# Accounting for ScalarE in the order of issue of a chain of Mamba layers

## The chip, the cores and the metric

The kernel runs on one core of one Trainium2 chip. The core has five engines with a queue each: TensorE (PE, with its weight loads shown as PEld), VectorE (DVE), ScalarE (ACT), GpSimd (POOL) and SyncE (SP, which here issues nearly all DMAs). The metric is the device time of one execution in microseconds (us); lower is better. Before the change it is 10859.94 us, the median of three runs (10855.66 to 10861.70).

## The reference

Four layers run one after the other on an input of 4 images, 192 channels, 64 x 64 pixels, all in float32.

- Layer 0: each image is 4096 tokens of 192 channels. They are normalised (mean and variance over the 192 channels, then scale and bias). Two Mamba blocks take the result, one of them with the channels reversed, and `out = xs + y1 + y2`.
- Layer 1: a layer norm, one Mamba block and a residual, then a depthwise 3 x 3 convolution with batch norm and gelu, a second layer norm and an MLP (192 to 768 to 192).
- Layer 2: a masked 3 x 3 depthwise convolution with weights made from the image means.
- Layer 3: a layer norm, a sedenion product in windows of 4 x 4 pixels, and an MLP.

A Mamba block is, in short:

```
xc, z = split(x @ in_w.T)                     # 384 channels each
xc = silu(conv1d(xc, conv_w) + conv_b)        # 4 taps (3 in layer 1)
dt, B, C = split(xc @ x_w.T)                  # 12, 16 and 16 columns
dt = softplus(dt @ dt_w.T + dt_b)
h[t] = exp(dt[t] * A) * h[t-1] + dt[t] * xc[t] * B[t]     # 16 states per channel
y = sum over the states of h[t] * C[t], + D * xc
out = (y * silu(z)) @ out_w.T
```

## The kernel before

**Tiles and units.** Tokens are cut into tiles of 512 (T), so there are 32 tiles. One tile of one Mamba block is a unit: layer 0 has 64 (the two blocks take turns), layer 1 has 32. The 384 channels by 16 states of a unit are laid out as 12 groups (k, 0 to 11) of 4 pieces (j) of 128 rows. So a unit is 48 scans, and the 48 scans of all units make one long stream. `Scans.run` goes through the stream one scan at a time; such a step is called a tick here.

**What a tick issues.** `Scans.step` puts out, for scan i: the decay two scans ahead (`decay`, L613: ACT computes `exp(dt * A)` into one of three PSUM tiles dA), and the scan itself (`step`, L619, DVE). After the last scan of a group (j = 3), `read` first copies the last column of h into the state kept for the next tile, and then multiplies h by C on POOL (L635). The state is copied by ACT in layer 0 (L632) and by POOL in layer 1 (L634). The next group's `product` follows (L606, dt * xc times B): DVE does it, except for groups 3, 7 and 11 of layer 0 ("shared"), which POOL does into buffers named h_apart. Some ticks later PE sums the states (`sum`, L644), and DVE takes the sums (`skip`, L667 in layer 0, L669 in layer 1). h has three buffers, h_apart two.

**All other work** runs behind the scans and is ordered by `Behind`. It holds lanes, queues of generators; each `yield Piece(...)` says what the next piece needs: time on PE (`pe`), ticks to wait (`wait`), flags that must be set (`after`), a PSUM bank (`bank`; two exist), or that it is a burst. A burst is an activation that needs another table than Exp (Silu, Softplus, Gelu), so that a table load stands before it and another one before the next decay. Bursts are let out only at an edge: the decay just issued is the last of a group and a product by DVE follows. At each tick `issue` first puts out evictions from PSUM that are due (2 ticks after the matmul for ACT in layer 0, 1 in layer 1; 3 and 2 for DVE); then the lanes are tried in order, as long as a budget of PE time per tick (`tile`: 1.85 in layer 0, 2.1 in layer 1) is above zero. Unused budget is not kept. `force` puts out everything that can go, with no regard to budget, until a condition holds: rows of dt in DRAM before they are loaded, C before the read, the gate's silu and a free y before `skip`.

**Layer 0's lanes.** Lane 0 spreads B and C. Lane 1 runs the fronts (`Mamba.front`): in_w product into raw, convolution (`convolve`) into xc, Silu burst (L471), x_w product, dt, Softplus burst (L495), dt and dt * xc to DRAM, z and its Silu burst (L513). xc has two buffers for both blocks together, so the convolution of a unit waits until the unit two places before it has done its `skip`. Lane 2 runs `back` (out_w, L871 to L888). Lane 3 runs `norm`: `bn_stats` and `bn_aggr` on DVE (L828, L829), four small POOL instructions for 1/sigma and shift (L832 to L835), four ACT passes of 128 x 192 (L839) and the transposes into xT, evicted by ACT (L853).

**Layer 1's lanes.** Lane 0: C and `back`. Lane 1: fronts (`sum_taps` replaces the convolution: three ACT evictions per projection, L559) and the first norm (`NormT.run`). Lane 2: `tail` with the depthwise convolution (L1101), its Gelu burst (L1120) and the second norm. Lane 3: the MLP (`MlpT.run`), with six evictions (L364), a Gelu burst over 3072 columns (L371) and the second product (L378). A tail waits for the MLP of three tiles before, and a back for that tile's second norm.

Layers 2 and 3 run from about 8960 us on with another scheduler (`Lanes`), which the diff leaves alone. `drain` issues what is left of layer 0 and layer 1 after their last scan.

Of the kernel before, what the change touches and what calls it, by code (L numbers as in the profile page):

```python
# [22 lines left out]
C = 192  # L23
# [141 lines left out]
class Piece:  # L165
# [4 lines left out]
    def __init__(self, pe=0.0, wait=0, after=(), burst=False, bank=False, lock=False):  # L170
        self.pe, self.wait, self.after, self.burst = pe, wait, after, burst
        self.bank, self.lock = bank, lock


class Behind:
# [4 lines left out]

    BANKS = 2

    def __init__(self, psum, tile, act, dve, lanes=4):
        self.psum, self.tile, self.act, self.dve = psum, tile, act, dve
        self.lanes = [deque() for _ in range(lanes)]
# [12 lines left out]
    def later(self, fn, dve=False, bank=True, more=0):  # L198
        done = [False]
        self.pending.append((self.now + (self.dve if dve else self.act) + more, fn, done, bank))  # L200
        return done

    def issue(self, everything=False):
        keep = []
        for entry in self.pending:
            due, fn, done, bank = entry
            if everything or due <= self.now:
                fn()
                done[0] = True
                self.held -= bank  # L210
            else:
# [3 lines left out]
    def try_lane(self, n, edge, force=False, idle=True):  # L215
# [11 lines left out]
        if not force and (self.now < self.ready[n] or (p.burst and not edge)):  # L227
            return None
        self.locked |= p.lock
# [9 lines left out]
    def tick(self, edge):  # L239
        self.now += 1  # L240
        self.issue()
# [13 lines left out]
    def force(self, until):  # L255
        while not until():
            self.now += 1
            self.issue(True)
# [3 lines left out]
    def drain(self, beside=lambda: None):  # L262

        while any(self.lanes) or self.pending:
# [4 lines left out]
class NormT:  # L269
# [15 lines left out]
    def run(self, x, g, b, d, which):  # L285
# [11 lines left out]
        yield Piece(after=[h], wait=3, lock=True)  # L297
# [20 lines left out]
        h = behind.later(power)  # L318
# [16 lines left out]
        yield Piece(after=[h], wait=3)  # L335
        for k in range(2):
            nc.scalar.activation(  # L337
# [4 lines left out]
class MlpT:  # L342
# [6 lines left out]
    def run(self, x, taken, last):  # L349
# [20 lines left out]
        yield Piece(after=made, burst=True)  # L370
# [31 lines left out]
class Mamba:  # L402
# [42 lines left out]
    def front(self, xn, first, u):  # L445
# [48 lines left out]
        yield Piece(after=halves, burst=True)  # L494
# [8 lines left out]
        yield Piece(1.7, bank=True, after=u["free"][1:])  # L503
# [8 lines left out]
        yield Piece(after=made, burst=True)  # L512
# [3 lines left out]
    def convolve(self, raw, project, u):  # L516
# [25 lines left out]
        yield Piece(after=halves, burst=True)  # L542

    def sum_taps(self, raw, projected, u):
# [3 lines left out]
        for d in range(ND):  # L548
            yield Piece(1.7, bank=True, after=u["free"][:1])
            if d == 0:  # L550
                xc = u["xc"] = self.work.tile([128, ND, T], F32, name="xc", bufs=2)
# [17 lines left out]
        yield Piece(burst=True, wait=4)  # L569
# [110 lines left out]
class Scans:  # L680
# [107 lines left out]
def two_mambas(tc, x, gb_ap, m_ins, ex_aps, out, at_first):  # L788
# [3 lines left out]
    with ExitStack() as ctx:  # L792
# [14 lines left out]
        behind = Behind(psum, 1.85, 2, 3)  # L807
# [12 lines left out]
        def norm(u):  # L820
            xt = u["x"]
            stats = work.tile([128, nq, 6], F32, name="stats")
            mv = work.tile([128, nq, 2], F32, name="mv")
            rs = work.tile([128, nq], F32, name="rs")
            for q in range(nq):
                if q == 2:
                    yield Piece(wait=1)
                nc.vector.bn_stats(stats[:, q, :], xt[:, q, :])  # L828
                nc.vector.bn_aggr(mv[:, q, :], stats[:, q, :])  # L829
            yield Piece(wait=1)  # L830
# [986 lines left out]
```

## Time and profile before

| | |
|---|---|
| median of three runs | 10859.94 us |
| the profiled execution, its own time | 10861.64 us |
| its span, first to last instruction | 10859.9 us |
| mean granted TensorE clock | 0.818 |
| layer 0's scans | 79 to 5321 us |
| layer 1's scans | 5418 to 8926 us |
| layers 2 and 3 | from about 8957 us |

| stretch of the span, us | PE | DVE | ACT | POOL busy |
|---|---|---|---|---|
| 82 to 5295 | 4257 | 5066 | 3535 | 4605 |
| 5430 to 8936 | 3025 | 2974 | 2282 | 2379 |
| 9200 to 10860 | 1442 | 833 | 667 | 171 |

All is of one profiled execution. Lines begin with the line of the kernel (L613), the engine and the operation; `out<-in` are the program's names for the tiles, then come shapes and the number of instructions, busy time in us, the mean duration of one in ns, and the idle time of the engine just before them with what ended it. ACT_TABLE_LOAD is a table load of ACT. PEclk is the share of its full clock that PE was granted.

### The profile page before, as it was taken

The page shows a single profiled execution, that of the slowest core. Times are in us where ns is not written, and L with a number is a line of the kernel's source. Part 1 is how long each engine was busy: PE and PEld are TensorE (multiplying, and loading weights), DVE is VectorE, ACT ScalarE, POOL GpSimd, SP SyncE. Part 2 cuts the span into 40 slices and gives each one's busy share as a digit, 9 for nine tenths or more (in the row PEclk, how much of TensorE's full clock was granted, in tenths as well). Part 3 has the DMA queues.
Part 4 walks back from the last instruction along what each step waited for, and adds up shares of the span by engine and source line. Part 5 has one row for each costly group of instructions (what it writes and reads, how often), then busy time and mean ns, then how long its engine had stood idle before and what let it go on. Part 6 is the DMA issues. An engine that isn't in the chain of part 4 may idle for free. (4 is left out here: it accounts for less than half of the span.)

```text
span 10859.9 us, 96522 instructions
## 1 busy us (share of the span) xinstructions
PE 9009.0 (83%) x30776; PEld 3561.5 (33%) x30776; DVE 9102.4 (84%) x7953; ACT 6632.6 (61%) x9880; POOL 7240.8 (67%) x2816
## 2 busy tenths in 40 slices
PE   7888888888888887887678889889888986889898
PEld 2222222222222222222223333333333323455455
DVE  8999999999999999999698888888888885555552
ACT  5666666666666666666466666666666653444443
POOL 6888888888888888888676666666676661111100
PEclk7777777777777777777678988888898887899999
DMA  6666666666666666666454545554454443112110
GB/s 170 174 181 179 174 182 176 174 182 177 177 180 181 177 175 184 175 178 181 128 149 129 140 128 135 138 134 135 131 145 129 132 110 81 41 50 64 43 40 18
DMA packets 969557, 1515.08 MB, mean 140 GB/s; under 512 B 244346, under 2 KB 277150, under 8 KB 968534
## 3 DMA queue, kind: packets, MB, share of 16 engines
q1 hardware_dynamic: 968190, 1505.85, 52.0%
q8 instruction: 243, 3.98, 0.2%
q10 hardware_dynamic: 856, 3.05, 0.1%
q14 instruction: 268, 2.20, 0.1%
HBM read 1295.45 MB, written 213.12 MB: 139 GB/s over the span
## 5 line engine op out<-in xcount | busy, mean ns | idle before, releaser
L619 DVE TENSOR_TENSOR_SCAN h<-dA,m_state,h 128x512 f32<-128x512 f32 x3840 | 4673.6, 1266 | 409.6 <-ACT dA L613 345.9
L635 POOL TENSOR_TENSOR h<-h,C 128x2048 f32<-128x2048 f32 x960 | 4347.4, 4534 | 605.3 <-ACT m_state L632 500.8
L613 ACT ACTIVATE dA<-dtE,m_A 128x512 f32<-128x512 f32 x4608 | 3108.4, 687 | 1468.6 <-DVE h L619 1370.2
L606 DVE TENSOR_TENSOR h<-dtxE,B 128x2048 f32<-128x2048 f32 x960 | 2169.4, 2260 | 67.1 <-DMA dtxE<-r_dtx 67.1
L644 PE MATMUL y<-h,gather 128*32 128x512 f32 x7680 | 1271.7, 740 | 472.4 <-POOL h L635 395.2
L1352 POOL TENSOR_TENSOR d<-d,rs 128x512 f32<-128x512 f32 x64 | 86.1, 1345 | 1613.2 <-DVE rs L1351 1592.7
L457 PE MATMUL ps_in<-xT,m_in_w 96*128 96x512 f32 x1536 | 942.1, 761 | 241.6 <-ACT raw L464 126.4
L619 DVE TENSOR_TENSOR_SCAN h_apart<-dA,m_state,h_apart 128x512 f32<-128x512 f32 x768 | 922.2, 1259 | 40.2 <-ACT dA L613 40.2
L606 POOL TENSOR_TENSOR h_apart<-dtxE,Bs 128x2048 f32<-128x2048 f32 x192 | 892.9, 4651 | 6.0 <-ACT Bs L595 6.0
L635 POOL TENSOR_TENSOR h_apart<-h_apart,C 128x2048 f32<-128x2048 f32 x192 | 870.7, 4535 | 38.7 <-ACT m_state L632 37.4
L531 PE MATMUL ps_conv<-raw,m_conv 128*128 128x512 f32 x1536 | 727.9, 625 | 0.0
L634 POOL COPY m_state<-h 128x4 f32<-128x4 f32 x384 | 71.9, 187 | 931.1 <-DVE h L619 891.4
L457 PE MATMUL ps_in<-xn,m_in_w 96*128 96x512 f32 x768 | 473.1, 767 | 230.4 <-ACT xc L559 148.2
L457 PEld LDWEIGHTS ps_in<-xT,m_in_w 96*128 96x128 f32 x1536 | 351.7, 242 | 811.5 <-issue 419.5
L644 PEld LDWEIGHTS y<-h,gather 128*32 128x32 f32 x7680 | 164.3, 116 | 1268.6 <-POOL h L635 582.2
L1101 PE MATMUL ps_dw<-strip,dw 96*96 96x512 f32 x1152 | 529.6, 609 | 1.6 <-ACT x L1110 0.9
L475 PE MATMUL ps_x<-xc,m_pack 128*44 128x512 f32 x576 | 353.2, 762 | 204.6 <-ACT xc L471 197.7
L1517 PE MATMUL sed_ps<-xn,sed 64*128 64x256 f32 (+3 forms) x2944 | 486.7, 404 | 7.0 <-DVE y L1536 7.0
L531 PEld LDWEIGHTS ps_conv<-raw,m_conv 128*128 128x128 f32 x1536 | 312.5, 207 | 449.4 <-issue 419.7
L613 ACT ACT_TABLE_LOAD x345 | 442.6, 1283 | 14.7 <-DMA dtE<-r_dt 8.6
L359 PE MATMUL ps_h<-xn,t 96*128 96x512 f32 x768 | 429.6, 715 | 15.0 <-ACT xn L337 9.8
L378 PE MATMUL ps_o<-hid,t 128*96 128x512 f32 x768 | 403.8, 673 | 27.5 <-ACT hid L371 23.3
(201 smaller groups left out, 12458.2 us busy)
## 6 DMA issues: line engine op xcount, KB each, us to landing
dtE<-r_dt SPq DMA_DIRECT2D x2304, 256.0 KB, 5.0
dtxE<-r_dtx SPq DMA_DIRECT2D x2304, 256.0 KB, 4.2
r_dt<-dt SPq DMA_DIRECT2D x96, 768.0 KB, 4.0
r_dtx<-raw SPq DMA_DIRECT2D x96, 768.0 KB, 5.4
x<-x SPq DMA_DIRECT2D x64, 384.0 KB, 3.9
img<-x SPq DMA_DIRECT2D x28, 512.0 KB, 8.3
xt<-in_x SPq DMA_DIRECT2D x32, 384.0 KB, 5.6
x<-o SPq DMA_DIRECT2D x32, 384.0 KB, 5.0
```

The source lines that it names most:

```text
L359: nc.tensor.matmul(ps, self.w1[:, k, bass.ts(m, 128)], x[:, k, :], start=(k == 0), stop=(k == 1))
L378: nc.tensor.matmul(ps, self.w2[:, m, bass.ts(k, CP)], h[:, m, :], start=(m == 0), stop=(m == NH - 1),)
L457: nc.tensor.matmul(ps, self.in_w[:, k, bass.ts(e, 128)], xn[:, k, :], start=(k == 0), stop=(k == 1))
L475: nc.tensor.matmul(ps, self.x_w[:, d, :], xc[:, d, :], start=(d == 0), stop=(d == ND - 1))
L531: nc.tensor.matmul(ps, self.conv[:, d, j, :], raw[:, d, j : j + T], start=(j == 0), stop=(j == K - 1))
L606: engine.tensor_tensor(h, u["rows", k // 2, 1], u[B, k % 2].unsqueeze(1).broadcast_to([128, 4, T]), ALU.mult)
L613: self.nc.scalar.activation(dA, u["rows", k // 2, 0][:, j, :], AF.Exp, scale=self.A[:, k, j : j + 1])
L619: self.nc.vector.tensor_tensor_scan(h[:, j, :], u.pop(("dA", k, j)), h[:, j, :], self.state[:, k, j : j + 1], ALU.mult, ALU.add,)
L635: nc.gpsimd.tensor_tensor(h, h, u["C", k % 2].unsqueeze(1).broadcast_to([128, 4, T]), ALU.mult)
L644: self.nc.tensor.matmul(u["ys"][32 * j : 32 * j + 32, :], self.ex.gather[:, i // 2, :], h[:, j, :], start=(i == 0), stop=(i == 3 and not s ...
L1101: nc.tensor.matmul(ps, dw[:, k, j, :], s[:, k, dy : dy + rows, dx : dx + HW], start=(j == 0), stop=(j == 8),)
L1517: nc.tensor.matmul(out, sed[p, int(h is not None), i ^ position(k, s), cols], xn[b, g][p, c, :], start=group(t) not in begun, stop=left[gr ...
```

## The change

- **An account of ScalarE.** `Behind` gets `spare`, the ACT time that a tick leaves free (1.0 in layer 0, 1.4 in layer 1; 0.7 more in `drain`). `left` rises by `spare` at each tick and never stands above it. Each ACT piece and eviction has a cost `act`, which is taken off. An ACT eviction that is due goes out only while `left` is above zero. A burst needs at least 0.6 of `spare`; another ACT piece needs its cost, or must be under 0.6 of `spare`.
- **Bursts first.** At an edge, one waiting burst is tried before the evictions that are due; before, the evictions came first.
- **PE's budget** per tick goes from 1.85 to 1.6 in layer 0 and from 2.1 to 1.8 in layer 1.
- **Layer 0's norm** takes its sums on ACT: four Identity passes that accumulate the sum, a POOL instruction that makes the negative mean, four Square passes with it as bias that accumulate the squares, three POOL instructions, and the four passes as before. `bn_stats` and `bn_aggr` go. Each pass is a piece of its own with a wait of one tick.
- **The state** is copied by POOL in layer 0 too.
- **xc** has three buffers: a convolution waits for the skip of the unit three places before. z keeps two.
- In the second part of `NormT.run`, each of the two last ACT passes is a piece.

```diff
-    def later(self, fn, dve=False, bank=True, more=0):
+    def later(self, fn, dve=False, bank=True, more=0, act=0.65):
         done = [False]
-        self.pending.append((self.now + (self.dve if dve else self.act) + more, fn, done, bank))
+        due = self.now + (self.dve if dve else self.act) + more
+        self.pending.append((due, fn, done, bank, 0.0 if dve else act))
         return done
 
     def issue(self, everything=False):
         keep = []
         for entry in self.pending:
-            due, fn, done, bank = entry
-            if everything or due <= self.now:
+            due, fn, done, bank, act = entry
+            if everything or due <= self.now and (not act or self.left > 0):
                 fn()
                 done[0] = True
                 self.held -= bank
+                self.left -= act
...
-        if not force and (self.now < self.ready[n] or (p.burst and not edge)):
+        if not force and (
+            self.now < self.ready[n]
+            or (p.burst and not (edge and self.left >= 0.6 * self.spare))
+            or (not p.burst and p.act > max(self.left, 0.6 * self.spare))
+        ):
             return None
+        self.left -= p.act
...
     def tick(self, edge):
         self.now += 1
+        self.left = min(self.left + self.spare, self.spare)
+        if edge:
+            for n in range(len(self.lanes)):
+                if self.says[n] and self.says[n].burst and self.try_lane(n, True):
+                    edge = False
+                    break
         self.issue()
...
     def force(self, until):
         while not until():
             self.now += 1
+            self.left = self.spare
             self.issue(True)
...
     def drain(self, beside=lambda: None):
 
+        self.spare += 0.7
...
-        yield Piece(after=[h], wait=3, lock=True)
+        yield Piece(after=[h], wait=3, act=1.05, lock=True)
...
-        h = behind.later(power)
+        h = behind.later(power, act=0.25)
...
-        yield Piece(after=[h], wait=3)
         for k in range(2):
+            yield Piece(after=[h], wait=0 if k else 3, act=0.8)
...
-        yield Piece(after=made, burst=True)
+        yield Piece(after=made, burst=True, act=5.3)
         nc.scalar.activation(h, h, AF.Gelu)
...
-        yield Piece(after=halves, burst=True)
+        yield Piece(after=halves, burst=True, act=4.1)
         nc.scalar.activation(dt, dt, AF.Softplus)
...
-        yield Piece(1.7, bank=True, after=u["free"][1:])
+        yield Piece(1.7, bank=True, after=u["z_free"])
...
-                    yield Piece(1.7 if j < K - 1 else 0.85, bank=j == 0, after=made + u["free"][:1])
+                    yield Piece(1.7 if j < K - 1 else 0.85, bank=j == 0, after=made + u["xc_free"])
                 if d == j == 0:
-                    xc = u["xc"] = self.work.tile([128, ND, T], F32, name="xc", bufs=2)
+                    xc = u["xc"] = self.work.tile([128, ND, T], F32, name="xc", bufs=3)
...
-        if self.shared:
-            nc.scalar.copy(self.state[:, k, :], h[:, :, T - 1])
-        else:
-            nc.gpsimd.tensor_copy(self.state[:, k, :], h[:, :, T - 1])
+        nc.gpsimd.tensor_copy(self.state[:, k, :], h[:, :, T - 1])
...
-            before = units[n - 2][1] if n > 1 else None
-            unit[1]["free"] = [before["skipped"], before["gated"]] if before else []
+            unit[1]["xc_free"] = [units[n - 3][1]["skipped"]] if n > 2 else []
+            unit[1]["z_free"] = [units[n - 2][1]["gated"]] if n > 1 else []
...
-        behind = Behind(psum, 1.85, 2, 3)
+        behind = Behind(psum, 1.6, 2, 3, 1.0)
...
-            for q in range(nq):
-                if q == 2:
-                    yield Piece(wait=1)
-                nc.vector.bn_stats(stats[:, q, :], xt[:, q, :])
-                nc.vector.bn_aggr(mv[:, q, :], stats[:, q, :])
...
+            def passes(func, sums=None, **args):
+                for q in range(nq):
+                    yield Piece(wait=1, act=0.55)
+                    more = {n: v[:, q : q + 1] for n, v in args.items()}
+                    if sums is not None:
+                        more["accum_out"] = sums[:, q : q + 1]
+                    nc.scalar.activation(xs[:, q, :], xt[:, q, :], func, **more)
+
+            yield from passes(AF.Identity, shift)
+            yield Piece(wait=2)
+            nc.gpsimd.tensor_scalar(shift, shift, -1.0 / C, None, ALU.mult)
+            yield Piece(wait=2)
+            yield from passes(AF.Square, rs, bias=shift)
+            yield Piece(wait=2)
+            nc.gpsimd.tensor_scalar(rs, rs, 1.0 / C, EPS, ALU.mult, ALU.add)
             nc.gpsimd.tensor_tensor(rs, rs, minus_half, ALU.pow)
-            nc.gpsimd.tensor_tensor(shift, mv[:, :, 0], rs, ALU.mult)
-            nc.gpsimd.tensor_scalar(shift, shift, -1.0, None, ALU.mult)
+            nc.gpsimd.tensor_tensor(shift, shift, rs, ALU.mult)
             yield Piece(wait=3)
...
+            yield from passes(AF.Identity, scale=rs, bias=shift)
...
-        behind = Behind(psum, 2.1, 1, 2)
+        behind = Behind(psum, 1.8, 1, 2, 1.4)
...
-            yield Piece(after=made, burst=True)
+            yield Piece(after=made, burst=True, act=3.6)
             nc.scalar.activation(x2, x2, AF.Gelu)
```

The two Silu bursts get `act=4.1` in the same way, and `sum_taps` the three buffers.

More of the change, by code (lines that the diff above doesn't have):

```diff
@@ L165, with __init__ @@
 class Piece:
-    def __init__(self, pe=0.0, wait=0, after=(), burst=False, bank=False, lock=False):
+    def __init__(self, pe=0.0, wait=0, after=(), act=0.0, burst=False, bank=False, lock=False):
         self.pe, self.wait, self.after, self.burst = pe, wait, after, burst
-        self.bank, self.lock = bank, lock
+        self.act, self.bank, self.lock = act, bank, lock
 class Behind:
     BANKS = 2
-    def __init__(self, psum, tile, act, dve, lanes=4):
+    def __init__(self, psum, tile, act, dve, spare, lanes=4):
         self.psum, self.tile, self.act, self.dve = psum, tile, act, dve
+        self.spare = self.left = spare
         self.lanes = [deque() for _ in range(lanes)]
@@ L511, in front @@
         u["xn_read"] = True
-        yield Piece(after=made, burst=True)
+        yield Piece(after=made, burst=True, act=4.1)
         nc.scalar.activation(z, z, AF.Silu)
@@ L541, in convolve @@
         nc.gpsimd.tensor_copy(self.halo, raw[:, :, T:])
-        yield Piece(after=halves, burst=True)
+        yield Piece(after=halves, burst=True, act=4.1)
     def sum_taps(self, raw, projected, u):
@@ L548, in sum_taps @@
         for d in range(ND):
-            yield Piece(1.7, bank=True, after=u["free"][:1])
+            yield Piece(1.7, bank=True, after=u["xc_free"])
             if d == 0:
-                xc = u["xc"] = self.work.tile([128, ND, T], F32, name="xc", bufs=2)
+                xc = u["xc"] = self.work.tile([128, ND, T], F32, name="xc", bufs=3)
                 one = self.work.tile([128, ND, 1 + T], F32, name="one", tag="dt", bufs=1)
@@ L568, in sum_taps @@
         nc.gpsimd.tensor_tensor(xc, xc, one[:, :, :T], ALU.add)
-        yield Piece(burst=True, wait=4)
+        yield Piece(burst=True, wait=4, act=4.1)
     def load(self, u, pair, i):
@@ L821, in norm @@
             xt = u["x"]
-            stats = work.tile([128, nq, 6], F32, name="stats")
-            mv = work.tile([128, nq, 2], F32, name="mv")
-            rs = work.tile([128, nq], F32, name="rs")
-            for q in range(nq):
-                if q == 2:
-                    yield Piece(wait=1)
-                nc.vector.bn_stats(stats[:, q, :], xt[:, q, :])
-                nc.vector.bn_aggr(mv[:, q, :], stats[:, q, :])
-            yield Piece(wait=1)
-            shift = work.tile([128, nq], F32, name="shift")
-            nc.gpsimd.tensor_scalar(rs, mv[:, :, 1], EPS, None, ALU.add)
+            shift, rs = (work.tile([128, nq], F32, name=n) for n in ("shift", "rs"))
+            xs = work.tile([128, nq, C], F32, name="xs", bufs=1)
+            def passes(func, sums=None, **args):
[12 more added lines that the diff above has]
+            nc.gpsimd.tensor_scalar(rs, rs, 1.0 / C, EPS, ALU.mult, ALU.add)
             nc.gpsimd.tensor_tensor(rs, rs, minus_half, ALU.pow)
-            nc.gpsimd.tensor_tensor(shift, mv[:, :, 0], rs, ALU.mult)
-            nc.gpsimd.tensor_scalar(shift, shift, -1.0, None, ALU.mult)
+            nc.gpsimd.tensor_tensor(shift, shift, rs, ALU.mult)
             yield Piece(wait=3)
-            xs = work.tile([128, nq, C], F32, name="xs", bufs=1)
-            for q in range(nq):
-                nc.scalar.activation(
-                    xs[:, q, :], xt[:, q, :], AF.Identity, scale=rs[:, q : q + 1], bias=shift[:, q : q + 1]
-                )
-                if q % 2:
-                    yield Piece(wait=1)
+            yield from passes(AF.Identity, scale=rs, bias=shift)
             xT = u["xT"] = work.tile([CP, 2, T], F32, name="xT", bufs=2)
@@ L1118, in tail @@
                 )
-            yield Piece(after=made, burst=True)
+            yield Piece(after=made, burst=True, act=3.6)
             nc.scalar.activation(x2, x2, AF.Gelu)
```

## The prediction

> **What bounds the kernel now.** I read the page's engine totals first, then busy time by stage. Core 0; start:end and length in us; busy us per engine; then granted TensorE clock, DMA share, GB/s:
>
> ```profile
> 82.00:5295.00 5213.00, 4257.22 (x13134) 1456.04 (x13138) 5066.26 (x4072) 3535.27 (x5712) 4604.60 (x1275) 0.77 0.66 178
> 5430.00:8936.00 3506.00, 3025.39 (x9004) 1095.73 (x9000) 2974.39 (x2311) 2281.85 (x3031) 2379.26 (x1295) 0.85 0.51 134
> ```
>
> Columns: PE, PEld, DVE, ACT, POOL. In layer 0 DVE works 5066 of 5213 us (97%), ACT 68%, POOL 88%. In layer 1 DVE works 85% and PE 86%: neither is full, so order costs time there. The last stage (9200 to 10860) doesn't use the changed scheduler. Next, DVE's groups in layer 0, then in layer 1 (busy us, mean ns, idle before and its releaser):
>
> ```profile
> L619 DVE TENSOR_TENSOR_SCAN h<-dA,m_state,h 128x512 f32<-128x512 f32 x2290 | 2766.7, 1264 | 102.3 <-ACT dA L613 64.1 <-DVE h L606 1.8
> L619 DVE TENSOR_TENSOR_SCAN h_apart<-dA,m_state,h_apart 128x512 f32<-128x512 f32 x764 | 917.4, 1259 | 40.2 <-ACT dA L613 40.2
> L828 DVE BATCH_NORM_STATS2 stats<-xt 128x6 f32<-128x192 f32 x124 | 41.0, 331 | 0.0
> L829 DVE BATCH_NORM_AGGREGATE mv<-stats 128x2 f32<-128x6 f32 x124 | 22.6, 182 | 4.3
> ...
> L619 DVE TENSOR_TENSOR_SCAN h<-dA,m_state,h 128x512 f32<-128x512 f32 x1530 | 1882.8, 1269 | 305.6 <-ACT dA L613 280.5 <-DVE h L606 0.5
> L330 DVE TENSOR_TENSOR xn<-xn,rb 96x1024 f32<-96x1024 f32 x61 | 73.5, 1205 | 31.9 <-PE rb L322 31.4
> L1136 DVE SCALAR_TENSOR_TENSOR x<-ps_o,t,x 96x512 f32<-96x512 f32 x58 | 43.3, 747 | 93.5 <-PE ps_o L378 93.5
> L1072 DVE TENSOR_TENSOR strip<-ps_out,x 96x512 f32<-96x512 f32 x62 | 42.6, 687 | 86.3 <-PE ps_out L1063 86.3
> ```
>
> Layer 0 loses 104 us waiting for decays and 64 us to the norm; layer 1 loses 280 us to decays and 211 us to late PE results. How layer 1 loses it shows in ACT's timeline (start, us, instruction, idle before):
>
> ```profile
> 6060.42 0.67 ACT L364 ACTIVATE hid<-ps_h,t 128x512 f32<-128x512 f32 x1
> 6060.99 1.29 ACT L613 ACTIVATE dA<-dtE,m_A 128x512 f32<-128x512 f32 x2
> 6062.30 1.28 ACT L371 ACT_TABLE_LOAD   x1
> 6063.60 2.77 ACT L371 ACTIVATE hid<-hid 128x3072 f32<-128x3072 f32 x1
> 6066.38 1.28 ACT L613 ACT_TABLE_LOAD   x1
> 6067.68 0.69 ACT L613 ACTIVATE dA<-dtE,m_A 128x512 f32<-128x512 f32 x1
> 6068.31 1.24 ACT L559 ACTIVATE raw<-ps_in,m_pack 128x512 f32<-128x512 f32 x2
> ```
>
> A table burst takes 5.4 us and two evictions stand behind each of the next decays. The pattern repeats every 109.2 us. In the period from 6000, DVE's waits add to 14.7 us; those from 6059 to 6090 (1.44, 1.41, 0.48, 0.48, 0.66, 0.43 for decays, then 2.87, 1.79, 0.70 for PE) are 10.3 of it. PE itself stood 6.99 us there for ACT's eviction of ps_in: that made ps_o and ps_out late.
>
> **What the skill says.** The Trainium skill, "ScalarE: Activation LUTs", section "What ACT_TABLE_LOAD costs", gives 1283 ns a load; the trace agrees (1283). It adds a drain of about 1380 ns; the trace shows none: 1.28 + 1.49 + 1.28 us stand end to end. "TensorE: Matmul & The Clock Gate", Part 1, says that an idle window of about 3.4 us halves the clock: after PE's 6.99 us of idling four ps_in matmuls took 3.78 us, against 1.88 before it. So a smoother order pays twice. "Perfetto Trace Analysis", section "Tensor Engine Instruction (MATMUL, LD_WEIGHTS)", calls ACT, DVE and GpSimd strict FIFOs: one instruction waiting at ACT's head holds every decay behind it. The trace agrees (ACT waited 25.3 us for shift, L835).
>
> **The change, part by part.** *bn statistics leave DVE.* Per tile 4 x (331 + 182) ns = 2.05 us; 31 tiles in the loop: 63.6 us, taken between scans, with 4.3 us idle. They hide behind nothing on DVE: gain 64, at most 68.
>
> *Eight passes join ACT.* The old pass (192 elements, two pointers) took 538 ns. The ScalarE page (same section) prices 186 + 0.833 per element + 93 per pointer: an estimate of 346 for the Identity sum, 439 for the Square, 532 for the old pass. No accumulator read of ACT is in the trace; I bound it by nothing and 190 ns (the short state copy, L632) and take 190. So 4 x 0.54 + 4 x 0.63 = 4.7 us per tile, 3.1 to 4.7. Square needs no load: layer 1's L299 runs between Exps without one.
>
> *State copies to POOL.* ACT loses 24 x 190 ns = 4.6 us per tile, and 162 us of waiting at L632 for scans (114.5 + 47.3), where evictions queued. ACT's total stays near 111 us of 163.8 per tile. POOL gains 24 x 0.26 us (start to start at L634 in layer 1) = 6.2 us per tile, minus a hop from ACT. POOL idled 615 us in layer 0, 19 per tile, so it stays under 96%. Only PE's y sums wait on POOL, and h has three buffers; cost nothing. Without that cover 6.2 x 32 = 200 us.
>
> *Norm's chain.* Its POOL work stays four small instructions (1.7 us), but ACT now waits on POOL twice, once for -mean with only two ticks between. POOL may be inside a 4.54 us read. Old: 0.8 us of ACT idle per tile. New: 0.8 to 4; ACT's next decays are behind it, but DVE holds two decays and often a product (2.26 us) as cover. I take 0.3 us of DVE wait per tile, 10 us; range 0 to 100. On POOL's side, the first of these instructions waits for ACT's last sum; behind it stand a read of h and an apart product, and for those only PE's sums wait, inside the same 19 us. By its waits the norm lasts 14 ticks longer (21 against 7), about 24 us.
>
> *Third xc buffer.* The convolution stalled for the skip: raw evicted at 3025, xc only from 3050; by my count of ticks the rows of the next unit were ready 5 to 9 us before use. Now the first front of a tile starts up to 24 us later, but doesn't stall some 23; the second only gains. So rows come no later, and PE and ACT work is spread more evenly. No time of its own; if rows came late, a forced issue per tile, as in D.
>
> *Account and bursts first.* Demand per layer 0 tile: 6 x 4.1 + 38 x 0.65 + 12 x 0.55 = 56 of 96 x 1.0; per layer 1 unit: 3 x 4.1 + 5.3 + 3.6 + 26 x 0.65 + 0.5 + 2.1 + 3.2 = 44 of 48 x 1.4. It fits. After a 4.1 burst evictions are held to the fourth tick in layer 0, to the second in layer 1 (gelu: third): the pile at 6068 can't form. In layer 0 I let 50 of the 104 us go (bounds 0 and 104): waits behind late PE remain. In layer 1, of the 10.3 us cluster half goes (5.1), and of two other burst waits (1.98, 0.66), whose bursts stood behind evictions, half (1.3): 6.4 us per unit. Bounds: nothing, and 13.
>
> *PE's budget, 2.1 to 1.8 in layer 1.* The pieces' own figures sum per unit to 83.7 us: front 10.2 + 2.6 + 2.55, C and spreads 3.4, sums 12.7, two norms 11, out 5.2, dw 15.6, mlp 20.4 (rounded). 48 x 1.8 = 86.4: 97% full, before 83%. Ticks in which both banks wait for an eviction are lost, so a backlog forms, and a forced issue throws it out in a clump. I charge 1.5 us per unit, between 0 and 10. In layer 0 it is 97.6 of 153.6: free. Lower pace also keeps PE from running behind DVE (1.93 us of DVE work per tick), so some charge is repaid.
>
> Sum: layer 0: -64 - 50 + 10 = -104. Layer 1: (-6.4 + 1.5) x 31 = -152. Drain and start: 0 (the drain's larger allowance acts on some 30 us). -256 from the profiled execution's 10861.6 (span 10859.9 + 1.7); the median, 10859.94, is the same within noise: 10604, said as 10605.
>
> **Rivals.** A, the forecast: both layers gain (10480 to 10700); for it, the exact repetition of the cluster, and ACT with a third of its time free. B: only layer 0 gains; the 97% budget gives back what layer 1 wins: 10861 - 104 = 10757 (10700 to 10838). For it, PE is as busy as DVE in layer 1. C: PE stays warm and all waits behind bursts go: -64 - 90 in layer 0, -9.5 x 31 = -295 in layer 1: 10412 (10340 to 10480). Against it, DVE and PE meet in too many places. D, slower: in layer 1 the budget starves the last lane (mlp); the tail, then the back, wait for it, and each unit ends in a forced issue that passes the account: several evictions and a burst ahead of the decays. Price 6 us per unit: 190 - 104 = +86, 10948; it decides once a unit grows by 3.4 us (104 / 31). Against it, a forced issue only takes what is missing. E: the order comes out nearly as before and POOL's waits eat the norm's gain: no change.
>
> **How the numbers follow.** A 0.51, B 0.17, C 0.11, D 0.17, E 0.04. 0.2% (10838 to 10882) is about what a measurement of this kernel tells from no change. A, B and C are faster: 0.79; E same: 0.04; D slower: 0.17. Range 10430 to 10890: it leaves out the better half of C (0.06) and most of D (0.13). The likeliest case's own range is 10480 to 10700.
>
> **What would show it.** Right: no L828 and L829; DVE's waits for dA in layer 0 about 55 us; the layer 1 period about 104 us, with no two evictions behind each decay after a burst, and PE's clock there above 0.85; L634 also in layer 0, POOL about 93%. Wrong: waits of ACT for shift or rs above 3 us per tile (norm); PE idle and then clumps in layer 1 (D); DVE waiting for h (POOL too slow).

## The result

The changed kernel takes 10810.36 us (median of four runs, 10802.70 to 10815.62) against 10857.80 us for the kernel before in the same series. The ratio is 0.9957, with a 95% interval of 0.9940 to 0.9974: 0.4% faster. The forecast was 10605 us. The profiled execution has a span of 10813.6 us (before 10859.9). Its stages, from the scans in DVE's timeline:

| | before | after | forecast of the difference | measured |
|---|---|---|---|---|
| layer 0's scans | 79 to 5321 us | 78 to 5423 us | -104 | +104 |
| layer 1's scans | 5418 to 8926 us | 5524 to 8882 us | -152 | -150 |

Layer 1 gained what was forecast. Layer 0 lost what it was to gain. The busy time by stage of the kernel after (start:end and length in us; busy us of PE, PEld, DVE, ACT and POOL; granted TensorE clock, DMA share, GB/s):

```profile
82.00:5400.00 5318.00, 4356.03 (x13137) 1464.87 (x13135) 5012.15 (x3825) 3556.11 (x5441) 4740.91 (x2039) 0.78 0.65 174
5540.00:8870.00 3330.00, 2960.45 (x8952) 1050.85 (x8952) 2952.79 (x2297) 2257.92 (x3013) 2359.28 (x1288) 0.87 0.53 141
```

DVE fell from 97% to 94% busy in layer 0 and rose from 85% to 89% in layer 1. Its groups in layer 0 and, below the dots, in layer 1 (busy us, mean ns, idle before and what ended it):

```profile
L636 DVE TENSOR_TENSOR_SCAN h<-dA,m_state,h 128x512 f32<-128x512 f32 x2291 | 2759.3, 1265 | 147.3 <-ACT dA L630 112.2 <-DVE h L623 0.5
L636 DVE TENSOR_TENSOR_SCAN h_apart<-dA,m_state,h_apart 128x512 f32<-128x512 f32 x764 | 920.8, 1262 | 50.6 <-ACT dA L630 50.4 <-POOL h_apart L623 0.2
L681 DVE TENSOR_TENSOR m_y<-y,z 128x512 f32<-128x512 f32 x190 | 130.5, 687 | 107.9 <-PE y L668 107.9
...
L636 DVE TENSOR_TENSOR_SCAN h<-dA,m_state,h 128x512 f32<-128x512 f32 x1521 | 1868.0, 1269 | 232.9 <-ACT dA L630 200.5 <-DVE h L623 0.9
L347 DVE TENSOR_TENSOR xn<-xn,rb 96x1024 f32<-96x1024 f32 x60 | 72.7, 1212 | 45.2 <-PE rb L339 45.2
L1150 DVE SCALAR_TENSOR_TENSOR x<-ps_o,t,x 96x512 f32<-96x512 f32 x58 | 43.2, 745 | 80.8 <-PE ps_o L395 80.8
L1086 DVE TENSOR_TENSOR strip<-ps_out,x 96x512 f32<-96x512 f32 x62 | 41.3, 666 | 8.8 <-PE ps_out L1077 8.8
```

The three rows of layer 0 and the missing batch-norm rows make up the loss. Waits for decays went from 104.3 to 162.6 us (+58). A new wait of the skip product for PE's y is 107.9 us. The statistics' 63.6 us are gone: 58 + 108 - 64 = +102. Counted in the traces, the waits for decays that end within 3 us of a table load on ACT grew in layer 0 from 44 to 93 us, and the others from 60 to 69: most of the +58 stands behind bursts. In layer 1 the waits for decays fell by 80 us, strip's by 77.5 and ps_o's by 13, and rb's rose by 14: -156, about the 150 measured. There the waits for decays behind table loads fell from 145 to 38 us, and the others rose from 137 to 164.

The y wait comes once per tile, at one unit's end. PE's timeline of the kernel after (start, us, instruction) shows what stands before y:

```profile
3012.02 2.07 PE L611 MATMUL ps_C<-dbl,spread 44*128 44x512 f32 x2 [0.35 <-ACT C L612]
3014.02 3.78 PE L474 MATMUL ps_in<-xT,m_in_w 96*128 96x512 f32 x4
3017.73 2.07 PE L611 MATMUL ps_Bs<-dbl,spread 44*128 44x512 f32 x2
3019.73 3.78 PE L474 MATMUL ps_in<-xT,m_in_w 96*128 96x512 f32 x4
3023.44 1.94 PE L658 MATMUL y<-h_apart,gather 128*32 128x512 f32 x8
3025.31 1.90 PE L668 MATMUL y<-xc,m_skip 128*128 128x512 f32 x2
3027.05 7.04 PE L548 MATMUL ps_conv<-raw,m_conv 128*128 128x512 f32 x16
3034.01 1.07 PE L658 MATMUL y<-h,gather 128*32 128x512 f32 x8
```

And DVE's timeline at the same place:

```profile
3021.42 2.26 DVE L623 TENSOR_TENSOR h<-dtxE,B 128x2048 f32<-128x2048 f32 x1
3027.25 0.69 DVE L681 TENSOR_TENSOR m_y<-y,z 128x512 f32<-128x512 f32 x1 [3.56 <-PE y L668]
```

PE has no gap from 3014 to 3034. Two projections of the next unit (ps_in, 3.78 us each) alternate with C and Bs, and y's last sums queue behind them. The skip is at the head of DVE's queue, the scans are behind it, and DVE stands 3.56 us. The matmuls here also run at about half the pace that PE has soon after: eight of y take 1.94 us before the wait and 1.07 us at 3034. All 27 waits for y of more than 3 us within layer 0's scans have such slow matmuls before them. By an estimate from the same matmuls at the quicker pace in this trace (1.98 us a projection, 1.12 Bs, 1.07 and 1.12 y), what stands from 3014 to 3027 would have taken 7.3 us in place of 13.0 if nothing else held it, and y would have been there before DVE came to it. So the order in PE's queue and PE's pace at this place hold DVE together; no run here parts them. The layer's mean clock doesn't show it (0.78 after, 0.77 before).

In layer 1 the pile behind the Gelu burst is gone. ACT's timeline of the kernel after, at the Gelu burst of the MLP:

```profile
6027.51 1.28 ACT L388 ACT_TABLE_LOAD   x1
6028.80 2.76 ACT L388 ACTIVATE hid<-hid 128x3072 f32<-128x3072 f32 x1
6031.59 1.28 ACT L630 ACT_TABLE_LOAD   x1
6032.88 1.91 ACT L630 ACTIVATE dA<-dtE,m_A 128x512 f32<-128x512 f32 x3
6034.73 0.24 ACT L332 ACTIVATE ln_rs<-var,eps 128x4 f32<-128x4 f32 x1
```

Three decays follow the table load at once, and so they do after all 29 Gelu bursts beside the scans. Before, one did and then two evictions, after 18 of 29. Here DVE waited 0.75 us for the first of them and for none of the rest.

ACT's groups in layer 0 for norm (busy us, mean ns, idle before) agree with the sum's prices:

```profile
L845 ACT ACTIVATE xs<-xt,shift,rs 128x192 f32<-128x192 f32 x124 | 67.0, 540 | 74.5 <-POOL shift L855 74.5
L845 ACT ACTIVATE xs<-xt,shift 128x192 f32<-128x192 f32 x124 | 54.9, 443 | 47.9 <-POOL shift L849 47.9
L845 ACT ACTIVATE xs<-xt 128x192 f32<-128x192 f32 x124 | 43.6, 351 | 0.0
...
L845 ACT ACTIVATION_READ_ACCUMULATOR xs<-xt 128x1 f32 x124 | 23.4, 189 | 0.0
```

### The profile page after: what moved, and what is told of

It reads as the page before. It is cut to its first block, busy times and chain, and to the rows that moved or that the text cites. A ratio compares the mean times of both kernels' runs of the same rounds, so it can differ in the third digit from the quotient of the medians.

```text
span 10813.6 us, 97520 instructions
## 1 busy us (share of the span) xinstructions
PE 9059.1 (84%) x30776; PEld 3532.3 (33%) x30776; DVE 9040.3 (84%) x7697; ACT 6650.6 (62%) x9626; POOL 7372.4 (68%) x3584
## 5 line engine op out<-in xcount | busy, mean ns | idle before, releaser
L474 PE MATMUL ps_in<-xT,m_in_w 96*128 96x512 f32 x1536 | 1141.5, 888 | 198.1 <-ACT z L481 175.1
L648 POOL COPY m_state<-h 128x4 f32<-128x4 f32 x960 | 180.9, 188 | 1182.7 <-DVE h L636 1175.2
L474 PEld LDWEIGHTS ps_in<-xT,m_in_w 96*128 96x128 f32 x1536 | 385.9, 275 | 968.3 <-issue 422.9
L1115 PE MATMUL ps_dw<-strip,dw 96*96 96x512 f32 x1152 | 590.5, 662 | 3.4 <-ACT x L1124 0.9
L474 PE MATMUL ps_in<-xn,m_in_w 96*128 96x512 f32 x768 | 440.6, 718 | 164.2 <-ACT z L481 70.5
L395 PE MATMUL ps_o<-hid,t 128*96 128x512 f32 x768 | 447.1, 730 | 76.2 <-ACT ln_rs L332 66.9
L548 PEld LDWEIGHTS ps_conv<-raw,m_conv 128*128 128x128 f32 x1536 | 285.3, 194 | 436.8 <-issue 345.7
L376 PE MATMUL ps_h<-xn,t 96*128 96x512 f32 x768 | 395.6, 662 | 30.2 <-ACT hid L381 16.7
```

The lines of the kernel that those rows point to most:

```text
L376: nc.tensor.matmul(ps, self.w1[:, k, bass.ts(m, 128)], x[:, k, :], start=(k == 0), stop=(k == 1))
L395: nc.tensor.matmul(ps, self.w2[:, m, bass.ts(k, CP)], h[:, m, :], start=(m == 0), stop=(m == NH - 1),)
L474: nc.tensor.matmul(ps, self.in_w[:, k, bass.ts(e, 128)], xn[:, k, :], start=(k == 0), stop=(k == 1))
L548: nc.tensor.matmul(ps, self.conv[:, d, j, :], raw[:, d, j : j + T], start=(j == 0), stop=(j == K - 1))
L1115: nc.tensor.matmul(ps, dw[:, k, j, :], s[:, k, dy : dy + rows, dx : dx + HW], start=(j == 0), stop=(j == 8),)
```

## Experiments

Times are medians; a ratio is to the kernel before in the same series, with its 95% interval. "The account" stands for the account and the bursts first, which every run keeps or leaves out together. Differences smaller than about 20 us aren't read.

**The layers apart (e1).** Layer 0 entirely as before, layer 1 as changed.

```diff
-behind = Behind(psum, 1.6, 2, 3, 1.0)      # layer 0
+behind = Behind(psum, 1.85, 2, 3, 1e9, first=False)   # and two xc, bn_stats, state on ACT
```

> Layer 0 is issued as before the change (statistics on DVE, state copied by ACT, two xc buffers, PE budget 1.85, no account, evictions ahead of bursts); layer 1 as after it. Theory: the change wins 150 us in layer 1 and loses 104 us in layer 0, and the two don't touch each other. Then this takes 10858 - 150 = 10708 us (10690 to 10730), layer 0's scans 5242 us, layer 1's 3360 us. Rival: part of layer 1's gain comes with layer 0's order (for instance through what the drain leaves); then 10740 to 10810 us.

10709.36 us, 0.9857 (0.9842 to 0.9872). Layer 0 ends at 5319 us and layer 1's scans take 3353 us. The layers hardly act on each other: layer 1's change is worth some 150 us, layer 0's costs 101.

**Layer 0: the third buffer and norm (e2, e3, e5).** e2 is the change with the statistics on DVE again; e3 the change with two xc buffers in layer 0; e5 has both edits.

```diff
-xc = u["xc"] = self.work.tile([128, ND, T], F32, name="xc", bufs=3)
+xc = u["xc"] = self.work.tile([128, ND, T], F32, name="xc", bufs=2)   # e3, e5; waits for units[n - 2]
-yield from passes(AF.Identity, shift)
+nc.vector.bn_stats(stats[:, q, :], xt[:, q, :])                       # e2, e5; and bn_aggr
```

> The changed kernel, with layer 0's norm as before: statistics on DVE, one POOL chain, four ACT passes. Theory N (the norm on ACT is what costs layer 0: it ends some 20 us later, so that the front it feeds starts at the unit's boundary with PE at half clock, and its passes stand in ACT's queue beside bursts): layer 0 falls from 5346 to 5180 to 5240 us although DVE does 64 us more, the wait of m_y for y (108 us) goes below 30 us, the total is 10650 to 10710 us. Theory X (third xc buffer), B (PE budget 1.6) or A (account): layer 0 rises by the 64 us of statistics, to some 5400 us, the total to some 10875 us.

> The changed kernel with two xc buffers in layer 0. Theory X (convolutions that no longer wait fall together with other PE work): layer 0 falls to some 5250 us, the total to some 10715 us. Theory N: the first front of a tile begins too late to wait for xc at all, so little changes there, and the second front loses its lead: 0 to 60 us slower, 10810 to 10870 us.

> The changed kernel with two xc buffers and the old norm in layer 0 (account, budget 1.6 and POOL's state copies stay). If the norm's move is worth what the prediction said once the third buffer is out of the way (64 us off DVE, some 10 us of waits for POOL), this is 54 us above the run with two buffers: 10700 us (10680 to 10720). Theory N (the norm on ACT costs more than it saves): below 10640 us.

| | norm on ACT | statistics on DVE |
|---|---|---|
| three xc | 10810.36 (the change) | 10710.47 (e2; 0.9860, 0.9845 to 0.9875) |
| two xc | 10644.43 (e3; 0.9801, 0.9784 to 0.9817) | 10796.68 (e5; 0.9941, 0.9925 to 0.9958) |

Either edit alone helps by 100 or 166 us, and both together by 14. The parts don't add up, so neither has a price of its own. Theory N foresaw e2, where y's wait is 14 us; theory X had the direction of e3, but not its size; e5 lies outside both branches written for it. DVE's rows in layer 0 of e3:

```profile
L636 DVE TENSOR_TENSOR_SCAN h<-dA,m_state,h 128x512 f32<-128x512 f32 x2300 | 2763.4, 1263 | 109.2 <-ACT dA L630 76.4 <-ACT xc L553 0.5
L636 DVE TENSOR_TENSOR_SCAN h_apart<-dA,m_state,h_apart 128x512 f32<-128x512 f32 x764 | 914.5, 1257 | 6.9 <-ACT dA L630 6.8 <-POOL h_apart L623 0.2
L681 DVE TENSOR_TENSOR m_y<-y,z 128x512 f32<-128x512 f32 x191 | 130.4, 683 | 33.0 <-PE y L668 33.0
```

Decays 83 us and y 33 us, 116 in all, against 271 in the change. Of these 155 us, y is 75; waits for decays behind a table load are 27 (93 to 67), and other waits for decays 53 (69 to 16). In e2 decays and y are 94 and 14, in e5 213 and 3.

**Where norm's end falls (e6, e12).** e6 holds the change's normed tile six ticks longer; e12 is e3 with a norm pass charged 0.65 instead of 0.55, so that it can't follow a burst directly (nor other work that leaves less than 0.65 in the account).

```diff
-            yield Piece(after=[h], wait=3)
+            yield Piece(after=[h], wait=9)            # e6
-                    yield Piece(wait=1, act=0.55)
+                    yield Piece(wait=1, act=0.65)     # e12
```

> The changed kernel, three xc buffers kept; only the last wait of layer 0's norm is 9 ticks in place of 3, so that the front behind it starts some 10 us later. Theory P (a collision: three raw projections of that front, at half clock, stand in PE's queue ahead of the last y sum at the unit's boundary, and the third buffer matters only because it moves the front there): the wait of m_y for y falls from 104 to below 40 us, layer 0 from 5346 to 5170 to 5260 us, the total to 10640 to 10725 us, although more waiting was put in. Theory X (early convolutions as such cost the time): layer 0 stays above 5320 us, the total above 10790 us.

> As the run with two xc buffers in layer 0 (10644 us), but each pass of norm is charged 0.65 of ScalarE's time instead of 0.55, so that it no longer passes the test at 0.6 of the spare directly after a burst. In that run one pass stood between a burst and the decays' table load once per tile or so, and a wait of 1.28 us for a decay followed (3075.4, 3235.0). If that pass causes the wait: waits for decays in layer 0 fall by 20 to 40 us, time 10605 to 10625. If the wait comes from the burst's length alone: 10635 to 10655. If it shifts norm onto another busy place: above 10660.

e6: 10808.60 us (0.9954, 0.9939 to 0.9969), with y's wait at 86 us in place of 108 and the decays' at 192 in place of 163: it only moved, against theory P, which had y's wait below 40 us once the front starts later. e12: 10798.37 us (0.9942, 0.9927 to 0.9957), 154 us slower than e3. Keeping the pass out of the burst didn't pay: norm's passes now stretch over 55 us of a tile (3127 to 3182) where e3's took 35 (3038 to 3073), y's wait is back once a tile (95 us), and the decays' is 172 us.

**PE's budget in layer 0 (e4, e13, e14).** The change with only this number altered.

```diff
-behind = Behind(psum, 1.6, 2, 3, 1.0)
+behind = Behind(psum, 1.85, 2, 3, 1.0)    # e4; 1.35 in e13, 1.2 in e14
```

> The changed kernel with layer 0's PE budget back at 1.85 a tick. Theory B (the lower budget holds PE work back until it collides with the unit's boundary): layer 0 falls by 50 to 100 us, the total to 10715 to 10765 us. Theory N or X: within 20 us of the changed kernel, 10790 to 10830 us, since the budget is only two thirds used.

> The changed kernel with layer 0's budget of PE at 1.35 a tick in place of 1.6 (the demand is 97.6 of 96 x 1.35 = 129.6 per tile, 75%). Theory G (PE gets ahead: with the third buffer the lanes always have work ready, the budget is spent each tick in microseconds of full clock, PE at its granted clock of 0.78 falls behind, and the y sums that stand in its queue come late; the run at 1.85 was 172 us slower): m_y's wait falls from 108 us to under 40 and the time to 10650 to 10730, with three buffers still in place. Theory S (the place where the convolution meets the boundary decides, whatever the rate): it lands somewhere between 10650 and 10900, with m_y's wait gone or above 80 us with no order by rate.

> As the run at 1.35, with the budget at 1.2 (demand 97.6 of 115.2, 85%). Theory G: as good as at 1.35 or better, 10630 to 10720. Theory S: no order by rate; 10650 to 10900. If the budget is too small for lanes to keep up, forced issues come and layer 0 grows: above 10850.

e4 10982.00 us (1.0112, 1.0097 to 1.0127), e13 10995.33 (1.0125, 1.0100 to 1.0150), e14 10987.37 (1.0118, 1.0103 to 1.0134). Both directions lose some 175 us, for different reasons; neither theory had said so of 1.85 or 1.35, and only a side remark, forced issues, of 1.2. At 1.85 the decays' waits are over 400 us. DVE's rows in layer 0 at 1.2:

```profile
L636 DVE TENSOR_TENSOR_SCAN h<-dA,m_state,h 128x512 f32<-128x512 f32 x2301 | 2765.1, 1263 | 61.9 <-ACT dA L630 20.9 <-DVE h L623 1.4
L636 DVE TENSOR_TENSOR_SCAN h_apart<-dA,m_state,h_apart 128x512 f32<-128x512 f32 x764 | 913.7, 1258 | 2.6 <-ACT dA L630 2.4 <-POOL h_apart L623 0.2
L681 DVE TENSOR_TENSOR m_y<-y,z 128x512 f32<-128x512 f32 x191 | 130.9, 686 | 431.8 <-PE ps_out L885 412.8 <-PE y L668 19.0
```

The decays' waits are nearly gone (23 us), and a wait for ps_out of 413 us is there. `back` stands in a later lane; the single y buffer is needed again before it has been issued, so `force` throws it out in one piece. PE's timeline of e13 at such a place:

```profile
3037.46 7.11 PE L474 MATMUL ps_in<-xT,m_in_w 96*128 96x512 f32 x12
3044.41 2.12 PE L885 MATMUL ps_out<-m_pack,m_y 128*128 128x192 f32 x12
3046.37 0.58 PE L894 MATMUL ps_out<-ident,xT 96*128 96x96 f32 x4
3046.79 2.15 PE L885 MATMUL ps_out<-m_pack,m_y 128*128 128x192 f32 x12
```

DVE's timeline of e13 has the price, 9.62 us once per tile:

```profile
3047.99 0.69 DVE L681 TENSOR_TENSOR m_y<-y,z 128x512 f32<-128x512 f32 x1 [9.62 <-PE ps_out L885]
```

This is rival D's mechanism, a lane starved by the budget and then forced, in the other layer.

**Does the y wait cost what it shows? (e9).** The change, with the skip of layer 0 due two ticks later.

```diff
-                self.at(i + 6 + late, lambda: self.skip(m, u, c))
-                self.at(i + 8, lambda: m.gate(u, c))
+                self.at(i + 6 + 2 * late, lambda: self.skip(m, u, c))
+                self.at(i + 8 + late, lambda: m.gate(u, c))          # gated() too
```

> The changed kernel, in which DVE's skip product of layer 0 (m_y <- y, z, at L681) is due two ticks later (10 instead of 8 after the last scan of its tile; the gate and what hangs on it come with it). DVE then has two more scans, 2.5 us, before it needs y. Theory W (the wait at m_y is itself the cost, and nothing else is late behind it): the 108 us of waiting for y in layer 0 fall under 25 us and the time by 85 to 105 us, to 10705 to 10725. Theory M (the cost is the order at the boundary: projections of the next tile between C, Bs and the convolution, which keep ScalarE waiting at its head for PE, so the decays are late as well): m_y's wait falls, the waits for decays grow by about as much, and the time falls by less than 40 us: 10770 to 10810.

10725.45 us, 0.9876 (0.9862 to 0.9891): 85 us less. DVE's rows in layer 0:

```profile
L636 DVE TENSOR_TENSOR_SCAN h<-dA,m_state,h 128x512 f32<-128x512 f32 x2300 | 2786.1, 1265 | 157.7 <-ACT dA L630 103.6 <-DVE h L623 0.9
L636 DVE TENSOR_TENSOR_SCAN h_apart<-dA,m_state,h_apart 128x512 f32<-128x512 f32 x767 | 920.3, 1257 | 43.1 <-ACT dA L630 43.0 <-POOL h_apart L623 0.2
L681 DVE TENSOR_TENSOR m_y<-y,z 128x512 f32<-128x512 f32 x191 | 126.8, 664 | 0.0
```

The y wait is gone and the waits for decays didn't grow by as much (147 us, before 163), so theory M falls. The time is at the upper edge of what theory W said: about half of what separates the change from e3 goes with this one wait. The decays' 147 us remain, though at other places: 54 us of them stand behind table loads, where the change has 93.

**The account in layer 0 (e10, e11).** The change, and e3, without account and bursts first in layer 0, at the same budget of 1.6.

```diff
-behind = Behind(psum, 1.6, 2, 3, 1.0)
+behind = Behind(psum, 1.6, 2, 3, 1e9, first=False)
```

> The changed kernel without the account and without bursts first in layer 0 (spare without limit, budget left at 1.6); three xc buffers and norm on ScalarE as in the change, layer 1 as in the change. Theory Acc (the account is what makes the third buffer bad together with norm's passes: twelve passes take 6.6 us of its time per tile, and evictions of the projections are held behind them): layer 0 falls back by 60 to 160 us, to 10650 to 10750. Theory Ord (the third buffer alone opens the projections at the boundary, whatever the account): 10790 to 10880, with m_y's wait still above 70 us.

> As the run with two xc buffers in layer 0 (10644 us), but without the account and without bursts first in layer 0. It measures their own part where the rest of layer 0 is smooth. The forecast's step gave the account 50 us of layer 0's waits for decays: 10694, between 10644 and 10748. The other theory, from layer 1, where the account without the smaller budget cost 73 us: the account gains nothing here either, 10600 to 10644.

e10 11013.02 us (1.0141, 1.0126 to 1.0156), outside what either theory said: with three buffers the account saves 203 us. Without it DVE waits 465 us for decays. e11 10574.61 us (0.9741, 0.9725 to 0.9758): with two buffers the account costs 70 us. e11 beats both kernels, by 2.6% and 2.2%. Its DVE rows in layer 0:

```profile
L637 DVE TENSOR_TENSOR_SCAN h<-dA,m_state,h 128x512 f32<-128x512 f32 x2301 | 2763.8, 1262 | 88.3 <-ACT dA L631 52.6 <-DVE h L624 0.9 <-ACT xc L554 0.5
L637 DVE TENSOR_TENSOR_SCAN h_apart<-dA,m_state,h_apart 128x512 f32<-128x512 f32 x768 | 920.1, 1258 | 15.0 <-ACT dA L631 12.9 <-POOL h L650 1.6
L682 DVE TENSOR_TENSOR m_y<-y,z 128x512 f32<-128x512 f32 x191 | 130.4, 683 | 0.0
```

Decays 65.5 us, y none: about what the forecast had expected of layer 0 (55 us), but without the account that was to bring it, and layer 0 ends at 5206 us, 115 before the old end; the forecast said 104. It has the new norm, the state on POOL and the smaller budget in layer 0, and neither the third buffer nor the account; which of the first three it needs was not run.

**A low rate with its fault removed (e15, e17, e18).** e15 is e11 at 1.35. e17 and e18 are e13 and e15 with a second y buffer for the first direction (e17 has one buffer less for the staging tile o).

```diff
+        self.ys = self.y_free = 2 if name == "m0" and shared else 1
-            self.behind.force(lambda: m.y_free)
-            m.y_free = False
+            self.behind.force(lambda: m.y_free > 0)
+            m.y_free -= 1                        # back() adds one; e17: o with one buffer
```

> The best kernel so far (two xc buffers and no account in layer 0, 10575 us) with layer 0's budget at 1.35 in place of 1.6. Theory G: no worse, 10540 to 10580, as there PE is little behind. Theory S: a change of rate moves the pattern off a good place: 10600 to 10750.

> The kernel with layer 0's budget at 1.35 (10995 us), with a second buffer for the first direction's y (m0_y), so that the first skip of a tile no longer has to force the out-projection of the tile before (that wait, 9.6 us once a tile, was 309 us; the out-projection's staging tile o gets one buffer instead of two to make room). If the low budget's only fault is that forced out-projection (theory G with the last lane starved): 10995 - 309 = 10686, 10660 to 10740. If the lane stays behind and the wait moves to the second direction's y or to the next tile's norm: above 10800.

> The kernel with two xc buffers, no account and budget 1.35 in layer 0 (10927 us) with the second buffer for m0_y; its wait for ps_out was 339 us. If that is its only fault: 10588, 10560 to 10620, about as good as at 1.6 (10575), since there DVE waits little for decays already. If the wait moves: above 10700.

e15 10926.86 us (1.0063, 1.0048 to 1.0078), with 339 us of waiting for ps_out. e17 10864.10 (1.0002, 0.9994 to 1.0011), e18 10777.93 (0.9925, 0.9908 to 0.9941). The second buffer wins back 131 and 149 us, not the 309 and 339 of the wait. In e17 the decays' waits rise from 53 to 254 us, in e18 from 58 to 242. Once `back` isn't forced, its evictions and matmuls take other places, and the decays wait there. So theory G, that PE's rate alone is at fault, falls.

**Layer 1's parts (e7, e8, e16).** e7 and e8 have layer 0 as before and three xc buffers in layer 1: e7 with the new budget and no account, e8 with account and bursts first and the old budget. e16 is e11 with two xc buffers in layer 1.

```diff
-behind = Behind(psum, 1.8, 1, 2, 1.4)
+behind = Behind(psum, 1.8, 1, 2, 1e9, first=False)    # e7
+behind = Behind(psum, 2.1, 1, 2, 1.4)                 # e8
-xc = u["xc"] = self.work.tile([128, ND, T], F32, name="xc", bufs=3)   # sum_taps
+xc = u["xc"] = self.work.tile([128, ND, T], F32, name="xc", bufs=2)   # e16; waits for units[n - 2]
```

> Layer 0 as before the change; in layer 1 PE's budget of 1.8 and three xc buffers, but no account and evictions ahead of bursts. The prediction charged the budget 1.5 us per unit: 10905 us. Rival: the lower budget, which keeps PE from running behind DVE, is what won the 150 us: 10700 to 10760 us.

> Layer 0 as before the change; in layer 1 the account, bursts first and three xc buffers, but PE's budget back at 2.1. The prediction gave the account 6.4 us per unit: 10660 us, so better than the 10708 us with both. Rival (the budget wins): 10820 to 10870 us.

> The best kernel so far (10575 us) with two xc buffers in layer 1 as well, so that the third buffer is nowhere. If the third buffer has no part in layer 1's gain of 150 us: 10565 to 10590. If it carries part of it, as the convolution's stall for the skip comes back: 10600 to 10700. If it costs there as in layer 0: below 10550.

e7 10793.26 us (0.9938, 0.9923 to 0.9953), e8 10933.14 (1.0068, 1.0053 to 1.0083), e16 10953.40 (1.0086, 1.0070 to 1.0103). Layer 1's scans take 3508 us before, 3435 in e7, 3583 in e8, 3353 with both (e1), 3332 in e11, and 3713 in e16. The third buffer with the budget gains 73 us, with the account it loses 75, with both it gains 155. Beside the buffer, then, the account adds 82 us of gain where the budget is there (e7 to e1), and the budget adds 230 where the account is (e8 to e1). Taking the third buffer away from all three costs 381 us. The buffer by itself wasn't run, so neither budget nor account has a price alone. The account does what it was made for in this layer: waits for decays that end within 3 us of a table load are 157 us in e7 and 37 in e1. DVE's rows in layer 1 of e16:

```profile
L637 DVE TENSOR_TENSOR_SCAN h<-dA,m_state,h 128x512 f32<-128x512 f32 x1523 | 1871.8, 1268 | 486.4 <-ACT dA L631 462.5 <-DVE h L624 1.8
...
L1087 DVE TENSOR_TENSOR strip<-ps_out,x 96x512 f32<-96x512 f32 x62 | 42.4, 684 | 91.1 <-PE ps_out L1078 91.1
```

PE's groups in the same stretch show PE itself waiting for ACT's evictions:

```profile
L475 PE MATMUL ps_in<-xn,m_in_w 96*128 96x512 f32 x744 | 427.5, 720 | 206.2 <-ACT xn L355 122.0 <-ACT z L482 73.0 <-ACT xc L577 11.2
...
L308 PE MATMUL mean<-x,mean_w 96*96 96x512 f32 x240 | 168.5, 841 | 122.4 <-ACT z L482 120.9 <-DVE xn L310 1.6
```

In e11 the norm's mean (L308) waits nowhere and takes 606 ns a matmul, not 841. PE and ACT wait for each other in turns here, and the decays sit in ACT's queue behind evictions whose matmuls are late. That the decays wait for this reason is read from these rows; why the later conv output brings PE into that turn stays open.

## Why the prediction was right and wrong

*The statistics leave DVE: -64.* Right as a term: 63.6 us of rows are gone and DVE's busy time in layer 0 fell by about 55 us. As a gain it isn't sure: with three buffers the kernel that keeps them is 100 us faster.

*Passes on ACT.* Sizes right: 351, 443 and 540 ns against 346, 439 and 532, the accumulator read 187 to 189 against 190 taken, and no table load for Square. *ACT waits for POOL: +10.* ACT waited 122 us for the shift, 3.9 us per tile, above the 3 us that the text named as the sign of trouble. DVE hardly feels it directly: of its waits for decays in layer 0 only 2 us end within 5 us of such a wait of more than 0.5 us. Whether it delays other work isn't shown; with two buffers ACT waits 43 us for the shift (e3) and 0 (e11), on the same norm.

*State copies on POOL cost nothing.* Supported: DVE waits 0.7 us for products in layer 0. No run undid this part alone, and POOL's share is 89%, not 93%.

*Third xc buffer: no time of its own.* This is the step that failed. In layer 0 it cost 166 us (change against e3), 438 without the account (e10 against e11), and gained 86 with the old norm (e5 against e2); in layer 1 it gained 381. The step asked only when rows come, that is, whether the new place of the conv is late. It didn't ask what stands in PE's queue at a unit's end: in the change, the projections of the next unit beside C, Bs and y. The wait for y there, 108 us in the change, was in no rival. It needs more than the buffer (14 us with the old norm, 1 without the account), it comes without the third buffer too (95 us in e12), and moving the front by six ticks (e6) took only 22 us of it and lengthened the waits for decays, so how the buffer brings it about is not shown.

*Account and bursts first: 50 of the 104 us go in layer 0.* This step failed as well. Decays' waits rose by 58, 49 of them behind table loads, the kind of wait that it was to remove. In this company the account still helped by 203 us; with two buffers it hurts by 70. A term of -50 has no meaning apart from the order that it acts on.

*Layer 1: -198 for the account, +46 for the budget.* The sum, -152, was measured as -150, and the signs named for it showed (period 104.9 us as 3358 / 32, clock 0.87). The attribution was wrong: beside the other two parts the account is worth 82 us and not 198, the budget gains 230 where it was charged 46, and without the third buffer, charged nothing, the layer is slower than before (3713 us against 3508). The account's term was also counted for all 31 units, while the pile that it was read from stands behind 18 of 29 Gelu bursts. The total was right by luck of its terms.

*Rivals.* B had the layers the wrong way round. D's forced issue shows in none of DVE's waits of the change, and the 97% budget of layer 1 gained; it did occur in layer 0 at 1.35 and 1.2, at 9.6 us per tile, though the budget is only 75% and 85% full there. The measured time lies inside the whole range, and inside B's, but by luck: no case had layer 0 losing and layer 1 gaining.

*What stays open.* The runs show where layer 0's loss is (y, 85 us on removal, and the waits for decays behind table loads, 49 us more than before; what lengthens these was not isolated), and that the buffer, the norm and the account each gain or lose by what the others are. No single quantity was found that orders the times of the kernels with another layer 0, from 10575 to 11013 us: neither PE's rate (1.2 to 1.85) nor norm's end (e6, e12) does so. In ten of the eighteen runs the time lay outside every range written before it, so the theories above name places in the trace better than they foretell times. PE's pace at a unit's end, half in every long wait for y of the change, was not varied on its own.

## What to carry to other kernels

Where an issue order is planned ahead and each engine runs its queue in order, the parts of a change have no prices of their own: three parts of this one (buffer, norm, account) changed sign with the company they were in, all within layer 0. Try each part alone and each taken away, as one run here (two buffers, no account in layer 0) gave 2.6% where the whole gave 0.4%. When a buffer is added, look at what its producer will now stand next to in the queue, not only at whether the consumer gets it in time.

## What the runs showed of the hardware

Each accumulating pass on ACT is followed by a read of the accumulator of its own, 187 to 189 ns for 128 x 1, which comes on top of the pass (351 or 443 ns). A Square between Exps needs no table load: from 3141 to 3144 us in the change three of norm's Squares alternate with decays, without a load between. The mean granted clock of PE in layer 0 was no guide to the time: 0.77 before and in e3, 0.78 in the change, 0.82 in e2. Nor did it give the length of a matmul: one of a projection took 760 ns on average before and 891 in the change, at about the same mean clock.
